# Adding a node's own rows at the ends of layer 0's blocks instead of in its first stage

## The chip, the cores and the metric

The kernel runs on one core of a Trainium2 chip. A core has five engines that run side by side and wait for one another through semaphores: TensorE (PE in the profile; its weight loads are PEld), VectorE (DVE), ScalarE (ACT), GpSimd (POOL) and SyncE (SP), which here only issues DMAs. The metric is the device time of one launch in microseconds, the median of several runs.

## What is computed

The kernel runs four graph layers over 2708 nodes with 512 features each. `adj` is a symmetric 0/1 matrix of which about 2.4% are ones. Only layer 0 and the beginning of layer 1 matter here. Layer 0, cut to its core:

```python
Ab = A > 0
keep = Ab & (jnp.cumsum(Ab.astype(jnp.int32), axis=1) <= 64)   # first 64 neighbours of each row
cnt = keep.sum(axis=1, keepdims=True)
nb_mean = (keep @ X) / jnp.maximum(cnt, 1.0)
xj = leaky_relu(nb_mean @ W_nb.T + b_nb)
xi = leaky_relu(X @ W_line.T + b_line)
x1 = layernorm(X + xi + jnp.where(cnt > 0, xj, 0.0))
```

The own rows X enter as the residual of the last line. Layer 1 is a mean over all neighbours with two weights and a combining weight, then relu, residual and layer norm; layers 2 and 3 are attention over the neighbours.

## The kernel before

The nodes are cut into 22 tiles of 128 rows; tile 21 has 20 rows. The kernel is written in a framework that places the semaphores and, at compile time, sorts each engine's instructions by their order in the program and by a model of when they can start. On the chip each engine then runs its own list in that order. Three tools fix an order by hand: `pe(...)` chains TensorE instructions, `tc.issue_after(ins)` puts a block's instructions behind `ins` on its engine, and generators (`yield`) spread side work over the steps of a main loop.

**Layer 0, first stage** (lines 275 to 324, about 0 to 226 us). For each tile t of X it makes two products on TensorE. The first, with W_nb (`wnT`), is split into a high and a low part, yH (L222, ACT) and yL (L223, DVE), which stay in SBUF for the blocks. The second, with W_line (`wlT`), gets its bias (L317), the leaky step (L186, called in line 318) and, in line 319, the tile's own rows `xs(t)`, all on DVE; the result `u` is stored to `r0_dram` by a DMA that POOL issues (L320). X's rows are loaded by SP (L164, in `fetched`) and transposed on TensorE (L124).

Beside this, 14 of the 22 rows of masks are handled, one in most turns of the loop. A mask is a [128, 2708] tile of `adj`, loaded by POOL (L241). ACT counts its ones (`count`, L246). DVE finds the first 64 in two halves (`place`): a running count (a scan, L252) and a multiplication (L255) for each half. The first half is put behind yL and the second behind `low`, the last DVE step of the tile's `u`. In the following turn TensorE transposes the mask (L264) and ACT writes it to `maskT` (L268).

**Layer 0, blocks** (lines 328 to 475, about 226 to 505 us). The 22 tiles form six blocks, tiles 20 and 21 first and then five blocks of four. For each block TensorE adds up `keep @ y` over 22 steps j, with yH and yL (L460); ACT makes the kept mask of a step (L335). A block's end (L473) scales the sums into `us[t]`. Its tiles are then finished by the generator `finish` during the first steps of the next block: per tile it loads r0 (SP), adds the bias b_nb (L380), the leaky step (L186), then adds r0 (L383) and the layer norm (L108 to L115), and stores the row tile to `x1_dram` (POOL, L385). The last block is finished in the loop of the next stage. A second chain of side work, `both`, runs through the same steps: the other eight masks (`other_masks`), then the product of layer 1's weights with the combining weight (`weights1`, whose weight rows come through `fetched` too), then vectors for the attention layers (`vectors`, L443 and L444).

**Layer 1, first stage** (lines 480 to 492, about 505 to 668 us): as layer 0's first, over x1. It has two products for each tile, yH and yL again, `u` to `z1_dram`, and a rewriting of `maskT` on DVE (L485).

**The row buffers.** All row tiles that `fetched` loads from its default pool, `rows`, share three buffers: X in layer 0's first stage (two tiles ahead of use), r0 in `finish`, the weight rows in `weights1`, x1 in layer 1's first stage. A load is issued by SP when a buffer's last reader is done. SP runs its list in order, so a load that has no buffer yet holds those behind it.

Of the kernel before, what the change touches and what calls it, by code (L numbers as in the profile page):

```python
# [30 lines left out]
def kernel(  # L31
# [9 lines left out]
    nc = tc.nc  # L41
# [8 lines left out]
    def rows(t):  # L50
        return min(P, N - t * P)

    def bcast(vec, n):

        return bass.AP(tensor=vec.tensor, offset=vec.offset, ap=[[0, P], [1, n]])
# [27 lines left out]
    r0_dram = dram.tile([N, D], F32, name="r0_dram")  # L83
# [36 lines left out]
    def transposed(pool, psum, src, n, name, order=as_it_comes):  # L120

        ps = psum.tile([P, KD, P], F32, name="ps_tr")
        for k in range(KD):
            order(nc.tensor.transpose(ps[:, k, :n], src[:, k * P:(k + 1) * P], ident[:n, :n]))  # L124
        dst = pool.tile([P, KD, P], F32, name=name)
        nc.scalar.copy(dst[:, :, :n], ps[:, :, :n])
        return dst

    def transpose_weight(room, psum, dst, src):

        for ki in range(KD):
            wr = room[ki]
            nc.sync.dma_start(wr, src[ki * P:(ki + 1) * P, :])
            ps = psum.tile([P, KD, P], F32, name="ps_tr")
            for ko in range(KD):
                pe(nc.tensor.transpose(ps[:, ko, :], wr[:, ko * P:(ko + 1) * P], ident))
            nc.vector.tensor_copy(dst[:, :, ki * P:(ki + 1) * P], ps)
# [8 lines left out]
    def weight():  # L146
        return weight_tile().rearrange("p k a c -> p (k a c)")[:, :KD * D].rearrange("p (k c) -> p k c", k=KD)

    def early(first, n, make):

        made = {}

        def get(i, **how):
            for j in range(len(made), min(i + first + 1, n)):
                made[j] = make(j, **how)
            return made[i]
        return get
# [4 lines left out]
    def fetched(src, t, n, pool=ahead, name="rows", bufs=None):  # L162
        x_ = pool.tile([P, D], F32, name=name, bufs=bufs or (3 if pool is ahead else None))
        nc.sync.dma_start(x_[:n], src[t * P:t * P + n, :])  # L164
        return x_[:n]
# [19 lines left out]
    def leaky(dst, u):  # L185
        return nc.vector.scalar_tensor_tensor(dst, u, 0.01, u, op0=OP.mult, op1=OP.max)  # L186
# [7 lines left out]
    with ExitStack() as phase:  # L194
# [19 lines left out]
        def bias(src):  # L214
            b = sm.tile([P, D], F32, name="bias", bufs=1)
            nc.scalar.dma_start(b, src)
            return b
# [3 lines left out]
        def keep_y(t, n, pm):  # L221
            highs[t] = nc.scalar.copy(yH[:n, t, :], pm[:n])  # L222
            return nc.vector.tensor_sub(yL[:n, t, :], pm[:n], yH[:n, t, :].bitcast(F32))  # L223

        def product(xT, n, w, which, order=as_it_comes):
            pm = ps_mm.tile([P, D], F32, name=f"pm{which}")
            for k in range(KD):
                order(nc.tensor.matmul(pm[:n], xT[:, k, :n], w[:, k, :], start=(k == 0), stop=(k == KD - 1)))  # L228
            return pm
# [9 lines left out]
        def load_mask(i, m):  # L239
            n = rows(turns[i])  # L240
            nc.gpsimd.dma_start(m[:n], adj[turns[i] * P:turns[i] * P + n, :], max_dma_last_dim=N * 2)  # L241
            return m

        def count(i, m):
            t, n = turns[i], rows(turns[i])
            nc.scalar.activation(m[:n], m[:n], AF.Sigmoid, bias=gate[:n], scale=STEP, accum_out=cnts[:n, t:t + 1])  # L246
# [10 lines left out]
        def turn(i, m, psum, order=as_it_comes):  # L257
            t, n = turns[i], rows(turns[i])
            for g0 in range(0, NT, G):
                g1 = min(g0 + G, NT)  # L260
                ps = psum()
                for j in range(g0, g1):
                    w = rows(j)
                    order(nc.tensor.transpose(ps[:w, j - g0, :n], m[:n, j * P:j * P + w], identb[:n, :n]))  # L264
                parts = [(P, g0, min(g1, FULL))] + ([(rows(FULL), FULL, NT)] if g1 > FULL else [])
                for w, a, b in parts:
                    if a < b:
                        nc.scalar.activation(maskT[:w, a:b, t * P:t * P + n], ps[:w, a - g0:b - g0, :n], AF.Sign,  # L268
                                             saturate=False)
                yield  # L270

        def rows_of(src):
            return early(2, NT, lambda t: fetched(src, t, rows(t)))

        with ExitStack() as ph:
            st = ph.enter_context(tc.tile_pool(name="l0a", bufs=1))
            wnT, wlT = weight(), weight2
            room = [maskT[:, G + k, :4 * D].bitcast(F32) for k in range(2 * KD)]

            xs = rows_of(x)
            xTs = early(0, NT, lambda t, order=as_it_comes: transposed(ahead, ps_tr, xs(t), rows(t), "xT", order))

            transpose_weight(room[:KD], ps_tr, wnT, l0_w_nb)
            lows = {}
            for t in range(2):
                xT = xTs(t, order=pe)
                lows[t] = keep_y(t, P, product(xT, P, wnT, 0, pe))
            transpose_weight(room[KD:], ps_tr, wlT, l0_w_line)  # L290
            b_line = bias(bcast(l0_b_line, D))
            masks = early(1, HERE, lambda i: load_mask(i, st.tile([P, N], BF16, name="m", bufs=3)))
            masks(0)
            nc.gpsimd.memset(maskT[:, NT - 1, :], 0.0)
            nc.gpsimd.memset(maskT[:, :, N:], 0.0)
            counted = turned = 0
            for t in range(NT):
                n = rows(t)
                if t > 1:
                    lows[t] = keep_y(t, n, product(xTs(t, order=pe), n, wnT, 0, pe))  # L300
                xT = xTs(t)
                if t + 1 < NT:
                    xTs(t + 1, order=pe)
                while turned < counted - (t + 1 < NT):
                    for _ in turn(turned, masks(turned), lambda: sums(BF16, (P, G, P)), pe):
                        pass
                    turned += 1
                now = counted < min(HERE, -(-(t - 1) * HERE // (NT - 5)))
                if now:
                    m, places = masks(counted), st.tile([P, N // 2], BF16, name="places", bufs=1)  # L310
                    with tc.issue_after(highs[t].ins):
                        count(counted, m)
                    with tc.issue_after(lows[t].ins):
                        place(counted, m, places, 0, 2)
                pm = product(xT, n, wlT, 1, pe)
                u = sm.tile([P, D], F32, name="u")
                nc.vector.tensor_add(u[:n], pm[:n], b_line[:n])  # L317
                leaky(u[:n], u[:n])
                low = nc.vector.tensor_add(u[:n], u[:n], xs(t))
                nc.gpsimd.dma_start(r0_dram[t * P:t * P + n, :], u[:n])  # L320
                if now:
                    with tc.issue_after(low.ins):
                        place(counted, m, places, 1, 2)
                    counted += 1
# [3 lines left out]
        with ExitStack() as ph:  # L328
# [47 lines left out]
            def finish(ts_, us):  # L376
                for t in ts_:
                    n, u = rows(t), us[t]
                    r0 = fetched(r0_dram, t, n)
                    nc.vector.tensor_add(u[:n], u[:n], b_nb[:n])  # L380
                    leaky(u[:n], u[:n])
                    yield
                    nc.vector.scalar_tensor_tensor(u[:n], u[:n], has[:n, t:t + 1], r0, op0=OP.mult, op1=OP.add)  # L383
                    layer_norm(sm, u[:n], n, u[:n])
                    nc.gpsimd.dma_start(x1_dram[t * P:t * P + n, :], u[:n])  # L385
                    yield
# [63 lines left out]
            for i, b in enumerate(cuts):  # L450
# [19 lines left out]
                for t in ts_:  # L470
                    n = rows(t)
# [7 lines left out]
            xs = rows_of(x1_dram)  # L479
            xTs = early(0, NT, lambda t: transposed(ahead, ps_tr, xs(t), rows(t), "xT"))  # L480
            for t in range(NT):
                n = rows(t)
# [6 lines left out]
                u = sm.tile([P, D], F32, name="u")  # L489
# [3 lines left out]
        with ExitStack() as ph:  # L493
            st = ph.enter_context(tc.tile_pool(name="l1b", bufs=2))
            for t in range(NT):
                n = rows(t)
# [11 lines left out]
                u = sm.tile([P, D], F32, name="u")  # L508
# [231 lines left out]
    def heads_attention(name, att, as_rows, meanwhile={}):  # L740
# [4 lines left out]
        with ExitStack() as ph:  # L745
# [127 lines left out]
            for r, (b, h0) in enumerate(runs):  # L873
# [30 lines left out]
                for i, (c0, c1) in enumerate(parts):  # L904
                    nc.scalar.copy(oT[:, i, :c1 - c0], po[i][:, :c1 - c0])
                late_steps = {j: todo[j] for j in todo if j >= NT}
                todo = finish(b, h0, pd[r % 2], pair, oT, r + 1 == len(runs))
                for j, steps in late_steps.items():
                    todo.setdefault(j - NT, []).extend(steps)
# [517 lines left out]
```

## Time and profile before

| | us |
|---|---|
| median of 3 runs | 3004.74 (3001.74 to 3009.93) |
| the profiled execution | 3005.91 |
| its span | 3004.1 |
| PE busy | 2890.8 (96% of the span) |
| DVE busy | 1997.4 (66%) |
| ACT busy | 1533.7 (51%) |
| POOL busy | 251.0 (8%) |

The page describes one execution. Its second part cuts the span into 40 slices of 75 us and gives each engine's busy share of a slice in tenths. Timeline lines have start, duration (both us), engine, source line, operation, output and inputs, shapes, and in brackets how long the engine had stood idle and what released it. Wait lines have who waited for whom, the total in us, how often, and the longest. TensorE's matmuls are pipelined and their ends are modelled, so a busy TensorE is not at its peak.

### The profile page before, as it was taken

How to read it: one execution, taken by the hardware profiler on the slowest of the kernel's cores; microseconds unless marked ns; L12 is line 12 of the kernel's file. 1: busy time of each engine (PE TensorE's matmuls, PEld its weight loads, DVE VectorE, ACT ScalarE, POOL GpSimd, SP SyncE). 2: the span in 40 equal slices, each digit the busy share in tenths (PEclk: the TensorE clock that was granted, in tenths of full speed). 3: DMA queues.
4: the chain of work that ended last, by engine and by line, in shares of the span. 5: the costliest groups of instructions: out<-in, count | busy, mean ns of one | idle time of the engine just before them, and what ended most of it. 6: DMA issues, size and time to landing. Idle time of an engine off the chain costs nothing.

```text
span 3004.1 us, 36497 instructions
## 1 busy us (share of the span) xinstructions
PE 2890.8 (96%) x14456; PEld 1608.9 (54%) x14456; DVE 1997.4 (66%) x2405; ACT 1533.7 (51%) x1774; POOL 251.0 (8%) x341
## 2 busy tenths in 40 slices
PE   7999999999999999999998999999989999999998
PEld 3447766448888333444466334434465555555555
DVE  5975638512334999999976999999953535444342
ACT  3545543113224999999955899999941000000001
POOL 1110101201110000000022000000310000000000
PEclk9999999999999999999999999999999999999999
DMA  4533325422222011111144111121061000000000
GB/s 110 114 87 64 88 74 139 131 64 84 85 73 80 31 49 39 37 48 46 32 132 131 39 39 39 41 64 36 32 176 40 4 25 15 25 14 15 14 22 20
DMA packets 117426, 180.05 MB, mean 60 GB/s; under 512 B 41042, under 2 KB 65507, under 8 KB 117246
## 3 DMA queue, kind: packets, MB, share of 16 engines
q1 hardware_dynamic: 88974, 116.47, 13.3%
q0 software_dynamic: 18160, 57.39, 6.7%
q10 hardware_dynamic: 10112, 3.77, 0.5%
q8 instruction: 116, 1.90, 0.3%
q14 instruction: 64, 0.52, 0.1%
HBM read 147.55 MB, written 44.65 MB: 64 GB/s over the span
## 4 chain that ended last, share of the span: by engine, by line
PE 66%; DVE 19%; issue 6%; ACT 5%; DMA 3%; POOL 1%; SPq 0%; DVEq 0%; POOLq 0%; ACTq 0%
PE po L895 15%; PE pn L1056 13%; DVE e L703 10%; PE acc L506 7%; PE pm L228 7%; PE pm L627 6%; PE pl L1031 5%; PE pl L1022 5%; PE acc L460 4%; ACT c L730 3%; PE pd L799 2%; DVE places L252 2%; PE ps_tr L124 1%; DVE maskT L485 1%; DMA x_dram<-rows 0%
## 5 line engine op out<-in xcount | busy, mean ns | idle before, releaser
L703 DVE SCALAR_TENSOR_TENSOR e<-v_bc,ucol,maskT 128x1408 f32<-128x1408 f32 (+3 forms) x804 | 1136.4, 1475 | 326.1 <-PE pn L1056 315.5
L730 ACT ACTIVATE c<-e,bcol 128x1300 fp8e4<-128x1300 f32 (+1 forms) x688 | 967.7, 1423 | 75.5 <-DVE e L703 30.0
L895 PE MATMUL po<-e,R 128*64 128x512 f32 (+2 forms) x4224 | 904.1, 547 | 30.9 <-DVE e L703 27.5
L895 PEld LDWEIGHTS po<-e,R 128*64 128x64 f32 x4224 | 338.8, 136 | 563.1 <-issue 396.5
L1056 PE MATMUL pn<-e,R 128*128 128x512 f32 (+1 forms) x1056 | 413.5, 542 | 0.0
L1056 PEld LDWEIGHTS pn<-e,R 128*128 128x128 f32 x1056 | 191.0, 190 | 199.3 <-issue 196.1
L1024 ACT ACTIVATE w<-pl,b 128x256 f32<-128x256 f32 (+1 forms) x88 | 40.9, 465 | 372.9 <-PE pl L1022 364.8
L460 PE MATMUL acc<-yH,kT 128*128 128x512 f32 x484 | 198.3, 410 | 4.9 <-ACT kT L335 4.9
L228 PE MATMUL pm<-w,xT 128*128 128x512 f32 (+1 forms) x384 | 177.2, 605 | 23.1 <-DVE yL L223 19.7
L460 PE MATMUL acc<-yL,kT 128*128 128x512 f32 x484 | 190.3, 393 | 0.0
L506 PE MATMUL acc<-yH,mf 128*128 128x512 f32 x484 | 188.5, 389 | 0.0
L506 PE MATMUL acc<-yL,mf 128*128 128x512 f32 x484 | 188.3, 389 | 0.0
L627 PE MATMUL pm<-w,xT 128*128 128x264 f32 (+1 forms) x704 | 169.7, 395 | 2.9 <-DVE R L656 1.2
L228 PE MATMUL pm<-weight,xT 128*128 128x512 f32 (+1 forms) x352 | 161.9, 603 | 2.7 <-DVE u L317 1.9
L1031 PE MATMUL pl<-lin,w 128*128 128x512 f32 (+1 forms) x352 | 157.4, 592 | 0.0
L1022 PE MATMUL pl<-lin 128*128 128x256 f32 (+1 forms) x704 | 153.4, 371 | 3.7 <-DVE lin L924 3.7
L1022 PEld LDWEIGHTS pl<-lin 128*128 128x128 f32 x704 | 129.2, 190 | 34.4 <-issue 15.8
L627 PEld LDWEIGHTS pm<-w,xT 128*128 128x128 f32 (+1 forms) x704 | 131.2, 192 | 28.6 <-issue 2.4
L503 ACT CAST mf<-maskT 128x1024 fp32r<-128x1024 fp8e4 (+1 forms) x66 | 64.4, 977 | 158.0 <-PE acc L506 147.9
L222 ACT CAST yH<-pm 128x512 fp32r<-128x512 f32 (+1 forms) x44 | 25.7, 585 | 233.5 <-PE pm L228 233.5
L113 POOL TENSOR_TENSOR ln_rs<-ln_rs,half 128x1 f32<-128x1 f32 x88 | 57.5, 654 | 1019.6 <-DVE ln_rs L112 884.2
L335 ACT ACTIVATE kT<-maskT 128x512 fp32r<-128x512 fp8e4 (+1 forms) x132 | 77.6, 594 | 118.1 <-PE acc L460 118.1
(215 smaller groups left out, 2763.6 us busy)
## 6 DMA issues: line engine op xcount, KB each, us to landing
rows<-x_dram SPq DMA_DIRECT2D x63, 256.0 KB
v_bc<-v_dram SPq DMA_DIRECT2D x16, 704.0 KB
x_dram<-u POOLq DMA_DIRECT2D x42, 256.0 KB, 2.4
v_bc<-v_dram SPq DMA_DIRECT2D x16, 650.0 KB
m<-in_adj_dram POOLq DMA_DIRECT2D x13, 677.0 KB, 8.5
rows<-in_x_dram SPq DMA_DIRECT2D x21, 256.0 KB
r_dram<-u POOLq DMA_DIRECT2D x21, 256.0 KB, 3.3
rows<-r_dram SPq DMA_DIRECT2D x21, 256.0 KB
```

The costliest lines, as they stand in the source:

```text
L228: order(nc.tensor.matmul(pm[:n], xT[:, k, :n], w[:, k, :], start=(k == 0), stop=(k == KD - 1)))
L335: made = nc.scalar.activation(kT[:, :w], maskT[:, j, b[0] * P:b[0] * P + w], AF.Relu, scale=-1.0)
L460: nc.tensor.matmul(pa[t], kT[:, (t - b[0]) * P:(t - b[0] + 1) * P], y[:, j, :], start=(j == 0 and y is yH), stop=(j == NT - 1 and y is yL))
L503: nc.scalar.copy(mf[:, :g1 - g0, :], maskT[:, g0:g1, t * P:(t + 1) * P])
L506: nc.tensor.matmul(pa, mf[:, j - g0, :], y[:, j, :], start=(j == 0 and y is yH), stop=(j == NT - 1 and y is yL))
L627: nc.tensor.matmul(pm[a][:m, :D // 2 + heads], xT[:, k, :m], w[:, k, a, :D // 2 + heads], start=(k == 0), stop=(k == KD - 1))
L703: self.made = nc.vector.scalar_tensor_tensor(e[:, :w], v[:, :w], ucol[:, j, h:h + 1], maskT[:, j, c0:c0 + w], op0=OP.max, op1=OP.mult)
L730: nc.scalar.activation(c[:, :w], e[:, :w], AF.Sigmoid, bias=bcol[:, j, h:h + 1], scale=STEP, saturate=False)
L895: pe(nc.tensor.matmul(po[i][HO * k:HO * k + HO, :c1 - c0], R2[:, j, h * HO:(h + 1) * HO], e[:, c0:c1], start=(i_ == 0), stop=(i_ == NT - 1)))
L1022: nc.tensor.matmul(pl[:, :w], self.lin1[:, k, f * P:(f + 1) * P], h[:, k, :w], start=(k == 0), stop=(k == KD - 1))
L1031: nc.tensor.matmul(pl[:n], gT[:, f, (t - t0) * P:(t - t0) * P + n], self.lin2[:, f, :], start=(f == 0), stop=(f == KF - 1))
L1056: nc.tensor.matmul(pn[k][:, :w], R2[:, j, k * P:(k + 1) * P], e[:, :w], start=(j == 0), stop=(j == NT - 1))
```

## The change

The add of X's rows leaves the first stage: `low`, behind which the second half of a mask is ordered, is now the leaky step itself, and what goes to `r0_dram` is xi alone. In `finish` each tile loads its rows of X again, beside r0, through the same three buffers, and adds them to r0 on DVE before r0 is added to the sums.

```diff
@@ first stage, for each tile t @@
                 nc.vector.tensor_add(u[:n], pm[:n], b_line[:n])
-                leaky(u[:n], u[:n])
-                low = nc.vector.tensor_add(u[:n], u[:n], xs(t))
+                low = leaky(u[:n], u[:n])
                 nc.gpsimd.dma_start(r0_dram[t * P:t * P + n, :], u[:n])
@@ finish, for each tile t of a block @@
-                    r0 = fetched(r0_dram, t, n)
+                    r0, x0 = fetched(r0_dram, t, n), fetched(x, t, n)
                     nc.vector.tensor_add(u[:n], u[:n], b_nb[:n])
                     leaky(u[:n], u[:n])
+                    nc.vector.tensor_add(r0, r0, x0)
                     yield
                     nc.vector.scalar_tensor_tensor(u[:n], u[:n], has[:n, t:t + 1], r0, op0=OP.mult, op1=OP.add)
```

## The prediction

> **What bounds the kernel now.** I read the page's 40 slices first, then busy time by stage, then VectorE's timeline in the first stage, then the waits of the Sync queue and of TensorE in the stages that follow.
>
> ```profile
> PE   7999999999999999999998999999989999999998
> DVE  5975638512334999999976999999953535444342
> ...
> 45.73:204.00 158.27, 140.02 (x608) 70.63 (x607) 147.55 (x134) 82.18 (x110) 16.78 (x27) 1.00 0.48 102
> 226.00:505.00 279.00, 271.84 (x1247) 204.86 (x1246) 165.16 (x244) 137.10 (x215) 30.53 (x43) 0.99 0.34 84
> 505.00:668.50 163.50, 160.78 (x436) 73.06 (x434) 72.25 (x109) 26.16 (x48) 26.01 (x30) 1.00 0.35 107
> ```
>
> The columns of the last three lines are: stretch in us, its length, then busy time (and instructions) of PE, weight load, DVE, ACT and POOL. TensorE is busy nearly everywhere, and DVE fills only some slices. The first stretch holds the 14 masks that are counted in layer 0's first stage: DVE is busy 147.6 of 158.3 us (93%) and PE leaves 18.3 us unused. In layer 0's blocks (226 to 505) PE leaves 7.2 us and DVE 114 us; in layer 1's first stage (505 to 668.5) PE leaves 2.7 us. The same microsecond of DVE work is therefore dear before 204 us and nearly free after 226 us.
>
> One turn of the first stage on DVE shows how strictly it is bound there:
>
> ```profile
> 127.78 0.68 DVE L317 TENSOR_TENSOR u<-pm,bias 128x512 f32<-128x512 f32 x1
> 128.49 0.69 DVE L186 SCALAR_TENSOR_TENSOR u<-u 128x512 f32<-128x512 f32 x1
> 129.22 0.69 DVE L319 TENSOR_TENSOR u<-u,rows 128x512 f32<-128x512 f32 x1
> 129.83 3.03 DVE L252 TENSOR_TENSOR_SCAN places<-m,places,over 128x1354 bf16<-128x1354 bf16 x1
> 132.78 0.67 DVE L223 TENSOR_TENSOR yL<-pm,yH 128x512 fp32r<-128x512 f32 x1
> 133.36 0.85 DVE L255 TENSOR_TENSOR m<-m,places 128x1354 bf16<-128x1354 bf16 x1
> 134.32 2.98 DVE L252 TENSOR_TENSOR_SCAN places<-m,over 128x1354 bf16<-128x1354 bf16 x1
> 137.33 0.87 DVE L255 TENSOR_TENSOR m<-m,places 128x1354 bf16<-128x1354 bf16 x1
> 138.11 0.68 DVE L317 TENSOR_TENSOR u<-pm,bias 128x512 f32<-128x512 f32 x1
> ...
> 133.59 3.67 PE L228 MATMUL pm<-w,xT 128*128 128x512 f32 x8 [1.27 <-DVE yL L223]
> 139.29 2.55 ACT L246 ACTIVATE m<-m,gate 128x2708 bf16<-128x2708 bf16 x1 [0.92 <-DMA m<-in_adj_dram]
> ```
>
> The turn repeats every 10.33 us (127.78 to 138.11) with no gap on DVE. The product on PE waits 1.27 us for yL (L223), which stands behind the second scan in DVE's order. The count on ACT waits for its mask, but ends at 142.0, well before the scan that needs it (144.65).
>
> The other side of the change, the row loads:
>
> ```profile
> SPq L164 <- DVE u L319: 184.5, 19, 21.7
> ...
> SPq L164 <- DVE u L383: 139.9, 16, 40.2
> ...
> PE pm L228 <- DMA w<-in_L_gnn_W_comb_dram: 2.0, 1, 2.0
> ...
> 397.48 3.92 SPq L164 DMA_DIRECT2D rows<-in_L_gnn_W_self_dram  x2
> 401.48 0.39 SPq L160 DMA_DIRECT2D w<-in_L_gnn_W_comb_dram  x1
> ```
>
> The Sync queue mostly waits for one of the three row buffers to be given back: by L319 in the first stage, by L383 in the blocks (times are total, count, longest). Once this already reaches PE: a row load stands until L383 at 400.3 frees its buffer, the weight load queued behind it leaves at 401.48, and PE's product waits for it until 407.26.
>
> [...] L319 shows 690, so the moved add costs the same in either place. [...] The trace has a shorter step than an instruction's duration, 0.60 to 0.61 us to an independent one, and 0.72 to one that needs the result (128.49 to 129.22). [...]
>
> **The change part by part.** The sum is made against the profiled execution: 3005.91 us around a span of 3004.1. That is 1.2 above the median of the runs, 3004.74, which I take off at the end.
>
> Removed: L319, 22 times. In 14 turns (tiles 2 to 6, 8 to 12, 14 to 17) the second scan is ordered behind it. In 12 of them DVE goes leaky, 0.72, add, 0.61, scan; without the add leaky, 0.61, scan: 0.72 saved. In two turns (60.8 and 108.5 us) small reciprocal steps already fill part of the gap, and 0.60 is saved. 12 x 0.72 + 2 x 0.60 = 9.84 us. The other eight (tiles 0, 1, 7, 13, 18 to 21) save nothing: there PE or the count on ACT ends last, as in DVE's 1.65 + 2.66 us of idleness around 100 us. What is late next in a turn: PE's wait falls from 1.27 to 0.55, so PE doesn't become the bound. The r0 store and the mask load behind it on POOL follow the leaky step now and move up with it; the mask's slack before its scan shrinks from 144.65 - 142.03 = 2.6 to about 1.9. So I take all of 9.8; the lower bound, if the mask loads or PE stop half of it, is 5.
>
> Also removed: the row buffer's last reader in the first stage was L319 and is now the transpose. Loads leave earlier; no PE wait of note hung on them, so nothing gained.
>
> Added: 22 loads of x0, 256 KB each (the last tile 40), issued by SP. They take 0.33 us of SP each, 7 us in all, on a queue that mostly waits. The bytes (5.4 MB) are nothing at a DMA share of 0.34. A row lands some 2.65 us after issue (355.79 to 358.4 for a weight row).
>
> Added: 22 adds on DVE at 0.60 to 0.72, some 14 us. 18 fall between 226 and 505, beside 114 us of idle DVE; the add doesn't need the block's sums, so it can run in idle time once its rows are there. Cost nothing on the path by themselves. If the cover were gone they would be 18 x 0.6 = 11 us.
>
> Changed: the buffers. A finished tile now holds two of three row buffers instead of one, and the next tile's x0 needs one back. Where x0 comes only when the preceding add or L383 lets go, each step is 2.65 + 0.7 + issue, about 3.7 us: three such steps are 11 us where four tiles' finishing now takes 15 (389.3 to 404.4), so mostly beside it, and finishing ends up to 3 us later. Behind it in DVE's order stand the scans of the next mask (359.07 to 367.84), and behind those PE's turn at about 371.9: 4 us of slack, just enough. What isn't covered is the weight load at 401.48: it is queued behind row loads which now find the buffers taken by x0. I put the wait of 2.0 us there at 4.5, so 2.5 lost. Bounds: 0 (the scheduler sorts the queue otherwise) and 13.4, if all four W_self rows hold PE for a landing and an add (4 x 3.35).
>
> In layer 1's first stage the last block's four tiles are finished while DVE has a backlog (no gaps to speak of from 459 to 555). Four adds are 2.4 us of it, and an add that waits for x0 holds yL behind it, for which PE waits 2.0 us in all now. yL has about 2 us of slack before the next product, so I take 1.5 lost; bounds 0 and 12 (3 us at each of four tiles).
>
> Sum: -9.8 + 2.5 + 1.5 = -5.8; 3005.9 - 5.8 = 3000.1 as profiled, 2998.9 as median: 2999.
>
> **Rivals.**
> A, all is hidden: the buffers never hold up PE after 226 us, and only the 9.8 counts, or 10.5 where the earlier row loads also ease the first stage. For it: 114 us of idle DVE and 7 us of idle PE in the blocks. Against: the 2.0 us wait at 407, which hangs on exactly this ring. 3004.7 - 9.8 = 2995, to 2994.
> B, slower: the Sync queue. Loads of W_self, W_comb and x1 stand behind x0 loads that wait for a buffer. With the upper bounds above the return is 13.4 + 12 = 25.4, so 3004.7 - 9.8 + 25.4 = 3020. It decides from a return of 9.8 on. For it: 139.9 us of Sync waits for L383 already, and a ring that isn't enlarged while its load doubles. Against: the slack of 4 us ahead of PE's turns, and 40 us between the last weights (464) and their use (504).
> C, the first stage doesn't speed up as it should: the mask loads or PE take over after half, 5 us, and the return of 4 stays: 3003.7. Against: slack of 1.9 and 0.55 us left after the cut.
>
> **How the numbers follow.** Forecast (returned in part) 0.44, A 0.32, B 0.15, C 0.09. A measurement of this kernel tells about 0.3%, 9 us, from no change: faster is below 2995.7, slower above 3013.8. The forecast lies between 2995.7 and 3003, so in the middle band. A straddles the edge: 0.30 of its 0.32 counts as faster, with gains beyond 9.8 from a changed order among them; the forecast's lower tail adds 0.08. B is slower in 0.13, its mild end and C stay in the band. Faster 0.38, same 0.49, slower 0.13. The range for 8 in 10 goes from 2993 to 3010: it takes in A, C and the mild end of B, and leaves out B's worst and a larger gain.
>
> **What would show it.** The turn on DVE should be 9.61 us, PE's wait for yL there about 0.55, and layer 0's blocks should begin near 216 instead of 225.6. In the blocks DVE's busy time should rise by some 11 us and PE's idle time stay under 12. The weight load should leave late relative to the block's L383s and PE's wait for W_comb be near 4.5. I am wrong in the first part if the turn stays above 10 us, and in the second if PE's waits between the start of the blocks and the end of layer 1's first stage change by anything but 2 to 6 us. From there on nothing should differ.

## The result and the profile after

The changed kernel takes 2999.42 us (median of 14 runs, 2995.79 to 3003.64), beside 3004.85 us for the kernel before (14 runs). The ratio is 0.9982 with a 95% interval of 0.9975 to 0.9990: a gain of 5.4 us, which can be told from none, but is less than the 0.3% that the prediction took as the smallest change to count.

Of the profile after, first the 40 slices of the page, then busy time by stage; the stretches hold the same work as the three shown of before.

```profile
PE   8999999999999999999998999999989999999998
DVE  6866639512334999999967999999944435445242
```

```profile
40.43:191.30 150.87, 139.43 (x608) 70.77 (x607) 137.36 (x118) 81.47 (x110) 16.93 (x28) 1.00 0.48 104
213.00:496.00 283.00, 273.92 (x1250) 206.09 (x1250) 174.44 (x261) 137.66 (x217) 33.10 (x43) 0.99 0.39 99
496.60:660.10 163.50, 160.76 (x432) 72.67 (x432) 76.32 (x113) 24.79 (x45) 20.38 (x30) 1.00 0.36 113
```

In the first stretch DVE has 118 instructions instead of 134 and is busy 10.2 us less, but the stretch is only 7.4 us shorter. In the blocks DVE is busy 9.3 us more and leaves 109 us; PE leaves 9.1 us instead of 7.2.

The profiled spans can't be subtracted. The first count of a mask, which opens the bound part of the first stage, begins anywhere from 36.5 to 42.1 us in the nine profiles of this study, and two profiles of the kernel before differ by 5.0 us there. So the reading goes by stretches between fixed points, worked out from the timelines of PE and ACT: A, from the first count's table load on ACT to the blocks' first product; B, to the start of the first scaling at the first block's end (L473 in the kernel before); C, to the first product of layer 1's first stage; D, that stage, to the first product over all neighbours (L506); E, the rest of the span. In us:

| kernel | first count at | A | B | C | D | E | A to D |
|---|---|---|---|---|---|---|---|
| before | 41.76 | 183.8 | 27.9 | 252.9 | 163.2 | 2334.6 | 627.8 |
| before, second profile | 36.76 | 183.8 | 26.7 | 255.4 | 163.1 | 2338.7 | 629.0 |
| changed | 36.46 | 176.4 | 32.2 | 251.6 | 163.9 | 2336.7 | 624.1 |
| stage1_only | 41.79 | 176.5 | 26.3 | 254.6 | 163.1 | 2337.6 | 620.5 |
| finish_only | 39.26 | 183.8 | 32.3 | 253.8 | 163.9 | 2336.4 | 633.8 |
| pin_add | 39.22 | 176.5 | 27.2 | 251.0 | 165.9 | 2336.7 | 620.6 |
| yl_first | 36.64 | 174.0 | 30.9 | 251.2 | 163.2 | 2337.9 | 619.3 |
| yl_pin_most | 42.11 | 174.0 | 28.8 | 250.8 | 164.0 | 2338.1 | 617.5 |
| yl_pool | 38.67 | 184.5 | 28.2 | 253.1 | 163.1 | 2337.6 | 628.9 |

The change takes 7.4 us from A, which agrees within 0.1 us between the two profiles of before. E differs by 4 us between these two, and the changed kernel lies between them. B and C need a second look, because PE doesn't run equally fast in them. Ten microseconds of B in the two profiles of the same kernel before (PE's busy time and instructions come first, the granted clock is the third number from the end):

```profile
235.62:245.62 10.00, 10.00 (x52) 7.64 (x51) 7.03 (x8) 5.27 (x10) 0.00 (x0) 0.83 0.01 2
230.62:240.62 10.00, 10.00 (x59) 7.67 (x58) 7.35 (x8) 6.42 (x12) 0.16 (x1) 1.00 0.01 2
```

In the first of them some matmuls follow one another at 0.43 us instead of 0.23. So each stretch is split here into the time in which PE stands idle and the time in which it is busy (worked out from PE's timeline, us):

| kernel | PE idle in B | in C | in D | PE busy in B | in C | in D |
|---|---|---|---|---|---|---|
| before | 3.7 | 4.2 | 2.0 | 24.2 | 248.6 | 161.2 |
| before, second profile | 4.1 | 5.0 | 2.2 | 22.6 | 250.4 | 161.0 |
| changed | 6.8 | 2.9 | 2.7 | 25.3 | 248.7 | 161.1 |
| stage1_only | 3.7 | 4.4 | 1.9 | 22.6 | 250.2 | 161.2 |
| finish_only | 7.9 | 5.2 | 2.8 | 24.3 | 248.6 | 161.1 |
| pin_add | 4.6 | 2.3 | 3.4 | 22.6 | 248.7 | 162.6 |
| yl_first | 6.4 | 2.7 | 2.2 | 24.5 | 248.4 | 161.0 |
| yl_pin_most | 4.6 | 2.3 | 2.9 | 24.2 | 248.4 | 161.1 |
| yl_pool | 4.1 | 4.5 | 2.0 | 24.1 | 248.5 | 161.1 |

The busy time of B, C and D together is 433.7 to 434.1 us in eight profiles and 435.1 in the changed kernel: the slow steps fall now in B, now in C or D, in the two profiles of before too. What the change costs is therefore read from PE's idle time. Beside the mean of the two profiles of before it grows by 2.9 us in B, falls by 1.7 in C and grows by 0.6 in D. Of the 4 to 5 us by which B is longer, some 3 are waiting. Whether the longer wait also brings on slow steps can't be told: they stand in B in all three kernels with the early addition, and in three of the six other profiles.

A turn of the first stage on DVE, from the timeline of the changed kernel:

```profile
119.60 0.69 DVE L186 SCALAR_TENSOR_TENSOR u<-u 128x512 f32<-128x512 f32 x1
120.21 3.03 DVE L252 TENSOR_TENSOR_SCAN places<-m,places,over 128x1354 bf16<-128x1354 bf16 x1
123.28 0.87 DVE L255 TENSOR_TENSOR m<-m,places 128x1354 bf16<-128x1354 bf16 x1
124.06 0.69 DVE L223 TENSOR_TENSOR yL<-pm,yH 128x512 fp32r<-128x512 f32 x1
124.66 2.97 DVE L252 TENSOR_TENSOR_SCAN places<-m,over 128x1354 bf16<-128x1354 bf16 x1
...
129.16 0.69 DVE L186 SCALAR_TENSOR_TENSOR u<-u 128x512 f32<-128x512 f32 x1
```

The turn is 9.56 us, and PE's wait for yL at 124.89 is 0.49. But two instructions have changed places: yL (L223) now stands behind the second half's multiplication (L255). Before, the scan at 129.83 was followed by yL and then by L255. Nothing in the edit asks for this; it is what the compiler's model made of the shorter list.

The head of the blocks, from the chain of waits of the changed kernel (start, duration, what):

```profile
209.14 7.04 DMA rows<-in_x_dram
...
216.46 0.06 DVE rows L381
...
217.07 0.68 DVE u L317
...
217.77 0.34 ACTq L216
...
218.22 0.42 ACT kT L334
...
218.68 7.28 PE acc L460 x20
```

And the same addition in DVE's timeline:

```profile
216.46 0.69 DVE L381 TENSOR_TENSOR rows<-rows 128x512 f32<-128x512 f32 x1 [6.95 <-DMA rows<-in_x_dram]
```

SP issues the load of X's row for tile 20 at 209.14. Its addition stands at the head of DVE for 6.95 us until the row is there. Behind it in DVE's list is the bias of the first stage's last tile (L317, at 217.07), which has nothing to do with X. When that bias is added, ACT issues the load of the next bias (L216) into the one buffer that this bias was read from, then makes the kept mask kT, and PE waits 3.63 us for kT in the middle of its sums. Here the bias begins 4.15 us after the blocks' first product (212.92 and 217.07), 0.61 after the addition's start; in the kernel before, which has no addition ahead of it, it begins 0.10 us after that product (225.62 and 225.72). So the wait for a row passed to an instruction that never reads it. Between 216 and 495 us DVE stands 61.0 us in 8 waits for such rows, 39.9 of them at once at 444.15. The one at the head is the only one that PE's waits show (3.63 us there, none behind the 39.9): here what stands behind the addition decided, not how long it stood.

PE's waits in the blocks (who waited for whom, total, count, longest), first in the kernel before from 226 to 505 us, then in the changed kernel from 216 to 495 us:

```profile
PE acc L460 <- ACT kT L335: 4.9, 7, 2.0
...
PE acc L460 <- ACT kT L334: 8.1, 8, 3.6
PE pm L228 <- DMA w<-in_L_gnn_W_comb_dram: 0.7, 1, 0.7
```

Waiting for kT went from 4.9 to 8.1. The wait for W_comb, which was to grow from 2.0 to 4.5, fell to 0.7. SP's list, in its timeline, says why:

```profile
391.23 0.33 SPq L164 DMA_DIRECT2D rows<-in_x_dram  x1
391.65 0.39 SPq L160 DMA_DIRECT2D w<-in_L_gnn_W_comb_dram  x1
395.14 1.12 SPq L164 DMA_DIRECT2D rows<-in_L_gnn_W_self_dram  x2
```

The W_comb load now stands ahead of the two W_self rows; before, it stood behind them (397.48, 401.48). It leaves 5.2 us before PE needs it instead of 3.8.

### The profile page after: what moved, and what is told of

Read it like the earlier page. It is cut to its first block, busy times and chain, and to the rows that moved or that the text cites. A ratio compares the mean times of both kernels' runs of the same rounds, so it can differ in the third digit from the quotient of the medians.

```text
span 2997.2 us, 36514 instructions
## 1 busy us (share of the span) xinstructions
PE 2889.4 (96%) x14456; PEld 1609.6 (54%) x14456; DVE 1997.0 (67%) x2405; ACT 1532.8 (51%) x1774; POOL 216.7 (7%) x341
## 4 chain that ended last, share of the span: by engine, by line
PE 63%; DVE 20%; issue 6%; ACT 6%; DMA 4%; POOL 0%; SPq 0%; DVEq 0%; POOLq 0%; ACTq 0%
PE pn L1056 13%; PE po L895 13%; DVE e L703 12%; PE acc L506 7%; PE pm L228 6%; PE pm L627 5%; PE pl L1031 5%; PE pl L1022 5%; PE acc L460 4%; ACT c L730 4%; DVE places L252 2%; PE pd L799 2%; DMA rows<-o_dram 1%; PE ps_tr L124 1%; DMA rows<-in_x_dram 1%
## 5 line engine op out<-in xcount | busy, mean ns | idle before, releaser
L228 PE MATMUL pm<-w,xT 128*128 128x512 f32 (+1 forms) x384 | 174.2, 596 | 14.9 <-DVE yL L223 12.8
L506 PE MATMUL acc<-yH,mf 128*128 128x512 f32 x484 | 188.4, 389 | 0.0
L506 PE MATMUL acc<-yL,mf 128*128 128x512 f32 x484 | 188.3, 389 | 0.0
```

What stands on the lines that cost most here:

```text
L506: nc.tensor.matmul(pa, mf[:, j - g0, :], y[:, j, :], start=(j == 0 and y is yH), stop=(j == NT - 1 and y is yL))
```

## The experiments

Theory after reading the two traces: the edit consists of two parts that add up, a gain in A and a return in B; the return is the addition's place in DVE's list. Rivals: the two parts depend on each other through the compiler's order, or the return comes from the buffers and Sync's queue whatever the order on DVE. (The expectations below call the theory C and its rival R; these are not the prediction's rivals.)

**before_again: the kernel before, profiled again.**

> The kernel before, unchanged, profiled once more. Theory C (the changed kernel's early start is TensorE's): the two profiles differ by 5.3 us before the first mask is counted (41.76 against 36.46 us), since in the profile of before two products ran slowly (6.55 and 5.40 us against 3.70). Then this profile shows the table load ahead of the first count anywhere between 36.4 and 42, with products of 3.7 us where it is early. Rival R (the change itself brings it, since X's rows leave earlier, at 13.84 instead of 34.98 us): the table load comes at 41.8 again.

It took 3006.32 us. DVE's 100 instructions from 2 us before the first count to 190 us behind it come in the same order in both profiles. Its A and D equal those of the first profile to 0.1 us; the first count's start, B, C and E differ by 5.0, 1.2, 2.5 and 4.1. Differences of this size in those columns are no reading; 7.4 in A is one, and so are 3 us of PE's idle time in B, which differs by 0.4 between the two profiles.

**stage1_only: the first part alone, with X's rows left out.**

```diff
-                    r0, x0 = fetched(r0_dram, t, n), fetched(x, t, n)
+                    r0 = fetched(r0_dram, t, n)
                     nc.vector.tensor_add(u[:n], u[:n], b_nb[:n])
                     leaky(u[:n], u[:n])
-                    nc.vector.tensor_add(r0, r0, x0)
```

> X's own rows are left out altogether: no add in the first stage, no x0 load and no add at the blocks' ends. Theory C: the first stage gains 7.4 us between the first count and the start of the blocks (14 turns of 0.72, less 0.9 at each of three tiles without a count, where yL now stands behind the mask's multiplication), and nothing comes back later: 7 to 8 us faster than before (ratio 0.9975), and about 2 us faster than the changed kernel at its median. Rival R: 12 us faster (ratio 0.996).

2996.78 us, ratio 0.9970 (0.9959 to 0.9982). A is 176.5 as in the changed kernel, B 26.3 and PE's idle time there 3.7 as in the kernel before.

**finish_only: the second part alone; X's rows are added in both places.**

```diff
-                low = leaky(u[:n], u[:n])
+                leaky(u[:n], u[:n])
+                low = nc.vector.tensor_add(u[:n], u[:n], xs(t))
```

> The first stage keeps its add and the blocks' ends load and add X's rows as well, so X is added twice. It is the price of the second half alone. Theory C: 3 to 5 us slower than before (ratio 1.0013), most of it at the head of the blocks, where the add for tile 20 waits on VectorE for its row and holds up the last tile's bias add. Rival R (three row buffers are too few): 7 us or more slower, spread over all blocks.

3008.08 us, ratio 1.0012 (1.0003 to 1.0020). A is 183.8, B 32.3, and PE stands idle 7.9 us in B: the return at the head is there without the gain. The two ratios multiply to 0.9970 x 1.0012 = 0.9982, that of the change, so the parts add up as far as these intervals tell, which leave room for some 4 us. PE's idle time in C is 5.2 us here and 2.9 in the changed kernel, so an interplay of that size isn't excluded. Part of it is the W_comb load. Here too it leaves ahead of the W_self rows and 5.2 us before PE needs it, but it lands after 7.0 us instead of 5.9, and PE waits 1.8.

**pin_add: the addition ordered behind its own tile's leaky step.**

```diff
-                    leaky(u[:n], u[:n])
-                    nc.vector.tensor_add(r0, r0, x0)
+                    lk = leaky(u[:n], u[:n])
+                    with tc.issue_after(lk.ins):
+                        nc.vector.tensor_add(r0, r0, x0)
```

> The changed kernel with the add of X's rows ordered behind the same tile's leaky step, so that it cannot stand on VectorE before the block's sums are there. Theory C: TensorE's wait of 3.63 us for the kept mask at the head of the blocks goes, as does VectorE's idle time of 61 us for these rows; 3 to 4 us faster than the changed kernel, 8 to 9 faster than before (ratio 0.997). Rival R (buffers): now x0 holds its buffer longer, so the loads behind it leave later; no gain, or 2 us lost.

2997.36 us, ratio 0.9979 (0.9970 to 0.9987). PE's waits in B, changed kernel and then pin_add:

```profile
PE acc L460 <- ACT kT L334: 6.8, 3, 3.6
...
PE acc L461 <- ACT kT L334: 4.6, 2, 3.0
```

With the same loads, the same additions and the same buffers the wait of 3.63 us behind the addition is gone, and the bias (215.79 in DVE's timeline) begins 0.1 us after the blocks' first product again; the 3.0 is a wait for ACT's count of the next mask. B falls from 32.2 to 27.2. Of these 5.0 us 2.2 are waiting, and that was the addition's place; 2.7 are PE's slow steps, which B doesn't have here. The times don't tell pin_add from the changed kernel: 3 to 4 us were expected, the medians differ by 2, and the intervals overlap. D grew from 163.9 to 165.9. The last block is finished in this stage, where PE now waits 2.4 us for yL at once and 1.0 for a row of x1, 0.7 us more in all; the other 1.5 are slow steps (the product at 503.43 takes 5.40 us on PE, the ones before and behind it 3.60). That the early addition was the better place there isn't shown by so little.

**yl_first: the second half's multiplication behind the next tile's yL again.**

```diff
-                        place(counted, m, places, 1, 2)
+                        cut = place(counted, m, places, 1, 2, later=True)
...
+                if cut:
+                    with tc.issue_after(lows[t].ins):
+                        cut()
```

With `later`, `place` gives the multiplication back as a function; `lows[t]` is the yL of the next tile.

> The changed kernel, with the second half's multiplication (L255) of a counted tile ordered behind the next tile's yL (L223) on DVE again, as the kernel before has it in most turns; nothing else. If the missing 2.4 us of the first stage come from yL's place (0.9 us at each of the three tiles without a count of their own, 7, 13 and 18), the stretch from the first count's table load to the blocks' first product falls from 176.4 to about 173.7 us, the scan behind the second skipped tile comes forward, and the head of the blocks keeps its 3 to 5 us of waiting for the row of X: 2996.7 at the median, ratio 0.9973. If the three tiles are late for another cause (the count on ACT, the mask loads), the stretch stays at 176.4 and the time at 2999.4.

2997.94 us (2996.7 was expected), ratio 0.9979 (0.9970 to 0.9989). A is 174.0 (173.7 was expected), 2.4 less than in the changed kernel and 9.8 less than before. The median alone wouldn't separate this from the changed kernel; A, which repeats to 0.1 us, does. DVE's timeline in this kernel:

```profile
119.57 3.03 DVE L252 TENSOR_TENSOR_SCAN places<-m,places,over 128x1354 bf16<-128x1354 bf16 x1
122.52 0.67 DVE L223 TENSOR_TENSOR yL<-pm,yH 128x512 fp32r<-128x512 f32 x1
123.10 0.85 DVE L255 TENSOR_TENSOR m<-m,places 128x1354 bf16<-128x1354 bf16 x1
```

The turn from leaky step to leaky step is 9.62 us (118.96 to 128.58), as long as with yL behind. What came back isn't in the turns that carry a mask. Each scan's start, counted from the first count's table load and compared with the same scan before, shows where (worked out from the timelines; us earlier than before):

| | changed | yl_first |
|---|---|---|
| last scan before tile 7 | 3.13 | 3.08 |
| first scan behind it | 2.21 | 3.08 |
| last scan before tile 13 | 5.87 | 6.58 |
| first scan behind it | 4.96 | 6.58 |
| last scan of the stage | 8.32 | 9.83 |
| the blocks' first product | 7.4 | 9.8 |

The changed kernel gives back 0.9 us at each of the three tiles without a mask of their own (7, 13 and, behind the last scan, 18), where PE and not DVE ends last: there yL, standing behind a multiplication of 0.86 us (L255 at 86.76 for tile 7), holds the product (PE waits 1.44 us for it at 88.37). yl_first gives back nothing.

**yl_pin_most: as yl_first, and the addition pinned in all blocks but the last.**

```diff
-                    leaky(u[:n], u[:n])
-                    nc.vector.tensor_add(r0, r0, x0)
+                    lk = leaky(u[:n], u[:n])
+                    with tc.issue_after(lk.ins) if ts_[-1] != cuts[-1][1] - 1 else nullcontext():
+                        nc.vector.tensor_add(r0, r0, x0)
```

> As yl_first, and the addition of X's row is ordered behind the same tile's leaky step in all blocks but the last, so that it can't stand at the head of DVE while its row is on the way; the last block keeps the compiler's order. If the return comes from the hoisted addition, the first block ends some 27 us after the blocks begin (32.2 in the changed kernel, 27.9 in the one before), and layer 1's first stage stays at 163.9 us instead of the 165.9 of pin_add: first stage -2.7, head -4.5, together about 2992.5 at the median, ratio 0.996. If the ring of row buffers itself is the cost, and the order on DVE only decides where it shows, the 4.5 us come back in a later block and the time is that of yl_first, about 2997.

2997.60 us, ratio 0.9968 (0.9957 to 0.9980): the lowest ratio of all, but not the 2992.5 that was expected, and its interval overlaps those of pin_add, yl_first and the changed kernel. The time alone doesn't decide against the rival, which had 2997. The stretches say more. A is 174.0 and D 164.0 as expected, B 28.8 and not 27. Beside yl_first, which differs by the pinning alone, PE's idle time falls from 6.4 to 4.6 in B and from 2.7 to 2.3 in C, and grows from 2.2 to 2.9 in D: 1.5 us in all. In the later blocks of C the wait doesn't come back, which speaks against the rival that the buffers are the cost and order only decides where it shows; for D, with 0.7, that stays open. A to D is 617.5, 6.6 less than in the changed kernel and 10 to 11 less than before.

What B keeps is 1.6 us of slow steps more than in pin_add (busy 24.2 instead of 22.6) and 0.5 to 0.9 us of waiting more than before. For the second, DVE's timeline:

```profile
216.26 0.68 DVE L323 TENSOR_TENSOR u<-pm,bias 20x512 f32<-20x512 f32 x1 [3.51 <-PE pm L228]
...
225.54 1.57 DVE L252 TENSOR_TENSOR_SCAN spare<-spare,over 128x677 bf16<-128x677 bf16 x1 [7.89 <-ACT spare L246]
```

The last tile's bias runs as soon as PE has its product. DVE then idles 7.89 us for ACT's count of the next mask, and PE's longest wait, 2.9 us (2.0 and 2.4 in the two profiles of before), is for kT from the same engine, ACT. In pin_add, whose DVE idles 7.86 us there, the count itself waits 1.29 us for its mask to land, 0.39 and 0.75 in the two profiles of before. That the second load of X delays the mask is not shown.

**yl_pool: as yl_first, but GpSimd adds X's rows in the first stage, and no second load.**

```diff
                 low = leaky(u[:n], u[:n])
+                nc.gpsimd.tensor_add(u[:n], u[:n], xs(t))
                 nc.gpsimd.dma_start(r0_dram[t * P:t * P + n, :], u[:n])
...
-                    r0, x0 = fetched(r0_dram, t, n), fetched(x, t, n)
+                    r0 = fetched(r0_dram, t, n)
-                    nc.vector.tensor_add(r0, r0, x0)
```

> As yl_first, but X's rows are added in layer 0's first stage by GpSimd, behind DVE's leaky step, and not in the blocks; no second load of X. GpSimd issues the store of r0 and the mask loads of this stage in the same order, so both wait for the addition. If DVE's turn is what binds and the return is all from the second load and its addition, both parts are gone: table load to blocks about 173.7 us, head of the blocks 27, sum about -10 against the kernel before: 2995 less the yL part, 2992.5, ratio 0.996. If GpSimd's addition takes some 2 us or more and holds the mask loads behind it beyond their slack of about 2 us, the turn on DVE grows again by what is over, up to 1 us in each of 14 turns, and the time is 2998 to 3006.

3006.71 us, ratio 1.0006 (0.9998 to 1.0014): the second branch of the expectation held, 0.7 us above its upper end, and all of the gain is gone. A is 184.5. POOL's timeline, two of the additions:

```profile
31.16 1.27 POOL L325 TENSOR_TENSOR u<-u,rows 128x512 f32<-128x512 f32 x1 [22.22 <-DVE u L186]
...
136.17 3.93 POOL L325 TENSOR_TENSOR u<-u,rows 128x512 f32<-128x512 f32 x1 [4.67 <-DVE u L186]
```

And two multiplications of DVE, the one beside the end of that addition second:

```profile
133.90 0.87 DVE L255 TENSOR_TENSOR m<-m,places 128x1354 bf16<-128x1354 bf16 x1
...
139.53 1.29 DVE L255 TENSOR_TENSOR m<-m,places 128x1354 bf16<-128x1354 bf16 x1
```

The addition at 31.16 takes 1.27 us while DVE stands still (31.08 to 34.15); the eight in turns without a mask take 1.26 to 1.28. In all 14 turns with a mask it becomes ready beside DVE's scan and takes 3.92 to 3.93. The scan beside the second one runs from 136.00 to 139.03, and 1.07 us later, at 140.10, the addition is done; the additions at 125.98 and 195.51 end 1.07 and 1.06 us after theirs (spans on POOL are rough, but the store behind it leaves at 140.40). So it looks as if most of it ran behind the scan; what holds it isn't shown. The multiplication at 139.53, beside the addition's last 0.57 us, takes 1.29 us, the one at 133.90, with no addition beside it, 0.87. The turn is 10.19 us instead of 9.62, the mask load behind the addition on POOL leaves 5.6 us after the leaky step's start (125.20 and 130.77) instead of 1.7 in the changed kernel (119.60 and 121.33), and DVE's waiting for a count rises from 8.8 us in 3 waits to 14.7 in 9.

## Why the prediction was right, and where its steps failed

The time came out as forecast, 2999.4 for 2999.0, but that is luck. Every term was off, and the errors cancel: +2.4 in the first stage, +2.9 at the head of the blocks, -4.2 for W_comb and -0.9 in layer 1's first stage make +0.2.

*The first stage, -9.84 us.* Measured: -7.4. The turn (9.61 forecast, 9.56 measured), PE's wait for yL (0.55 and 0.49) and the 14 turns were right; PE, the mask loads and the count didn't take over. The step that failed is "The other eight (tiles 0, 1, 7, 13, 18 to 21) save nothing": three of them lost 0.9 us each, since the compiler put yL behind the multiplication; small gains elsewhere made up 0.3 of it. With yL back in its place yl_first has the forecast 9.8. I had costed the removal with DVE's order unchanged.

*The additions in the blocks, nothing.* This step failed, and it is the main one: "it can run in idle time once its rows are there. Cost nothing on the path by themselves." The idle time was there. That the addition costs the same in either place was an estimate from the first stage, and it held: L319 has a median of 691 ns, L381 of 687. But at the blocks' head the bias of the first stage's last tile stood behind the addition in DVE's list and began only 0.61 us after it, when the row was there, at a price of 2.9 us of PE's idle time in B (4.0 in finish_only). finish_only shows the price without the gain of the first stage, and pin_add that the place makes it: 2.2 us of it go. In layer 1's first stage I did reckon with an addition that holds yL behind it; at the head of the blocks, where the first load of X must come in anew, I didn't.

*The ring and the wait for W_comb, +2.5 us.* The wait fell from 2.0 us (2.7 in the second profile) to 0.7, and PE's idle time in C by 1.7, since the compiler "sorts the queue otherwise", the lower bound of that step; the bound was put at 0, and the sorting brought a gain. Sync did wait for the additions to give buffers back, 14.9 us in 12 waits of 2.4 at most, and none of it reached PE in the rest of the blocks. W_comb's own share was never tried by itself.

*Layer 1's first stage, +1.5 us.* Measured +0.6 to 0.8, and not by the way that was named. PE waits for yL as long as before (1.9 and 2.0 us). Only one of the four additions there waited for its row, 1.70 us at 557.66. What is new is one wait of 0.8 us for `u` (L490) at 524.87; why that step runs later stays open.

*The sum.* -7.4 in A and +2.9, -1.7 and +0.6 of PE's idle time in B, C and D make -5.6, beside -5.4 by medians and the forecast -5.8. By whole stretches A to D is 3.7 and 4.9 us shorter than in the two profiles of before, with 1.1 us more of PE's busy time in it. The sign that the prediction set itself, PE's waits from the start of the blocks to the end of layer 1's first stage growing by 2 to 6 us, came out at its lower edge: +2.5 against the first profile of before and +1.2 against the second. From there on nothing differs: E is 2336.7, between 2334.6 and 2338.7.

*The rivals.* A, all hidden, is off for the change as made by the 2.9 us at the head; yl_pin_most comes nearest to it, with a ratio that stands for 9.6 us (6 to 13). B, the Sync queue, didn't come: the waits rose on SP and not on PE. C had the amount of the first stage's loss too high (5 instead of 2.4) and the wrong cause: neither mask loads nor PE took over.

## What to carry to other kernels

Work moved to an engine with idle time wasn't free here, since it waited for a load: the addition stood 6.95 us at the head of DVE, and the bias behind it began 4.15 us after the blocks' first product instead of 0.10. Ask what stands behind such a step in the engine's list. Pinning it behind the instruction whose result it joins is a cure to try; here it took away 2.2 us of waiting. After any edit to a kernel with a compile-time order, compare the order of the instructions that weren't touched; here such shifts made 2.4 us of loss in one stage. Read differences of a few us by stretches between fixed points, against a second profile of the same kernel, and with PE's idle time apart from its busy time: half of what B lost by the pinning was PE's own speed.

## What the runs showed of the hardware beyond this

- The start of the program is not the same from execution to execution. In three of the nine profiles (the second of before, the changed kernel, yl_first) the early products of TensorE all take 3.6 to 3.7 us, and the first count begins at 36.5 to 36.8 us. In three (finish_only, pin_add, yl_pool) one of them takes 5.1 to 5.4 us, and it begins at 38.7 to 39.3. In the other three two of them take 5.4 to 6.6 us, and it begins at 41.8 to 42.1. The granted clock is 0.83 from 25 to 35 us in the first profile of before and 1.00 from 20 to 30 us in its second.
- A row of X (256 KB) issued 0.7 us behind a mask load of 677 KB landed after 7.0 us, where a weight row had taken 2.65. That the mask load is the reason wasn't tried.
- More than three row buffers weren't tried.
